# First gram by transposes, an early start for the second image's rows, three banks for the first mixing products, and weights made off VectorE

## The chip, the cores and the metric

The kernel runs on one core of a Trainium2 chip. The metric is the device time of one execution in microseconds; before the change three runs took 2819.15 to 2820.23 us, with a median of 2819.88 us. The engines are called by short names: PE is TensorE (matrix products), PEld its weight loads, DVE is VectorE, ACT is ScalarE, POOL is GpSimd, and SP issues most of the DMA transfers.

## The reference

The input x is 16 images of 64 channels with 128 x 128 pixels in float32. Four layers follow one another. Each normalizes its input over groups of two channels (`_gn`) and adds what it makes to its input:

```python
x = x + _L0_conv_ref(_gn(x), L0_conv_conv_w)    # gram over pixels, times the image, then a 1x1 convolution
x = x + _L1_conv_ref(_gn(x))                    # |Sobel x| + |Sobel y|
x = x + _L2_conv_ref(_gn(x), W, b)              # channels shifted left/right, 3x3 convolution, bias
x = x + _L3_conv_ref(_gn(x), w_bin, w1x1, b1x1, gamma, beta)  # 3x3, 1x1, batch norm over all images, clip
```

The core of layer 0 is

```python
gram = jnp.einsum('bcn,bdn->bcd', xf, xf) / N
y = jnp.einsum('bcd,bdn->bcn', gram, xf)
out = jnp.einsum('oc,bchw->bohw', conv_w, y)
```

so for each image a 64 x 64 gram matrix over its 16384 pixels is needed before any pixel of layer 0 can be made. The batch norm of layer 3 needs sums over all 16 images, so the last step over all pixels stands at the end.

## The kernel before

The work is a train of images (b = 0 to 15), each cut into NS = 8 chunks of R = 8 rows. An image lies on the 128 partitions as 64 channels times two halves of its rows. A loop over `step` (line 911), with four quarters q in each, runs the stages side by side on different images: `Front` (layer 0's product and layer 1, Sobel) starts with image 0 at step 15, `Layer2` at step 25, `Layer3` at step 35 (line 861); each image follows 8 steps behind the one before. A stage's method `at(i, q)` is called for its chunk i, which may be negative in the steps that prepare it. All instructions issued through `pe`, `dve`, `act`, `sp` and `pool` are kept in program order on their engine by the class `InOrder`, which is why nearly every instruction of the profile has line 73; one that waits holds all behind it on its engine.

**Gram** (line 407) makes the gram matrix. It loads the image as `xr`, eight tiles with the image row h on the partitions and eight channels each, in rows of 512 bytes (line 420, on SP). ACT copies each into `xw` with channels and columns exchanged (line 425). Then 128 small products on PE, one for each image column, add up the gram in PSUM (line 437), with a column of ones for the sums. A first image takes steps 0 to 9 for this. `pace` (line 871) gives the steps: image 0 from step 0, image 1 from step 12 at double speed, image 2 from step 16.

**gram_chain** (line 301) turns the gram into the mixing matrix `abd` and the coefficients `co` of the following normalization. It is a chain of tiny products and DVE instructions, a generator: each `yield` hands over, and `tick()` takes it one link further at the end of each quarter. It has two square roots on ACT (in `rstd`, line 257).

**Front** (line 450) loads x again in its own layout (line 463), mixes it by `abd` with `small_product` into one PSUM bank `po` (line 470), and ACT normalizes from there into `xh` (`prepare`, line 475). As `po` has one bank, each product waits until ACT has emptied the one before. `sobel` (line 527) is eight long DVE instructions (`u`, `e`) and two absolute values on ACT for each chunk; the first needs rows of the chunk itself and the first row of the next. For the first chunk of an image Front also stores a row of zeros from `w0` to DRAM (line 491, on SP).

**The weights** are prepared at the very start (lines 204 to 240): memsets on POOL, loads on ACT's queue, nine products `wb` x `w1` in three rounds on PE, and DVE copies and sums into `w3`, `w2`, `wm` and the packed forms `pk2`, `pk3`. The products share one region of the PSUM tile `bank`, so a round waits until the one before is copied out. The constants are loaded by SP ahead of everything (lines 118 to 133).

PSUM has the pools `ps_two` (two tiles of two banks each, for layers 2 and 3), `ps_one`, `ps_po`, `ps_g` and `ps_sm`. The SBUF pool `ring` holds `v2` (3 buffers), `v3` (2), `x3` (10), `y` and others, none of which is used before step 23.

Of the kernel before, what the change touches and what calls it, by code (L numbers as in the profile page):

```python
# [10 lines left out]
F32 = mybir.dt.float32  # L11
# [97 lines left out]
def tile_kernel(ctx: ExitStack, tc: tile.TileContext, x, cw_h, w2_t, b2, wbin_t, w1_t, b1, gamma, beta, consts, out):  # L109
# [6 lines left out]
    small = ctx.enter_context(tc.tile_pool(name="small", bufs=4))  # L116

    kc = cpool.tile([P, K_END], F32, name="kc")
    nc.sync.dma_start(kc, consts)

    def k(name):
        return kc[:, AT[name][0]:AT[name][1]]

    def load_const(src, shape, name):
        t = cpool.tile(shape, F32, name=name)
        nc.sync.dma_start(t, src)
        return t

    cwh = load_const(cw_h, [P, C], "cwh")
    b2_sb = load_const(b2, [P, 1], "b2_sb")  # L130
    b1_sb = load_const(b1, [P, 1], "b1_sb")
    gamma_sb = load_const(gamma, [P, 1], "gamma_sb")
    beta_sb = load_const(beta, [P, 1], "beta_sb")
    bn_sum = cpool.tile([P, B * NS], F32, name="bn_sum")
    bn_sq = cpool.tile([P, B * NS], F32, name="bn_sq")

# [56 lines left out]


    xw = wpool.tile([P, W // 2, C + 1, 2], F32, name="xw")
    nc.gpsimd.memset(xw[:, :, C, :], 1.0)

    xh = wpool.tile([P, 3, R + 2, W + 2], F32, name="xh")
    nc.gpsimd.memset(xh, 0.0)
    junk = wpool.tile([P, R * W], mybir.dt.bfloat16, name="junk")  # L200
    wbd = wpool.tile([P, P], F32, name="wbd")
    nc.gpsimd.memset(wbd, 0.0)

    w2 = wpool.tile([P, 3, 3, P], F32, name="w2")
    w3 = wpool.tile([P, 3, 3, P], F32, name="w3")
    nc.gpsimd.memset(w2, 0.0)
    nc.gpsimd.memset(w3, 0.0)
    for slot, i, o, ky in TO_SLOTS:
        nc.scalar.dma_start(w2[i * C:(i + 1) * C, slot, :, o * C:(o + 1) * C], w2_t[:, ky])

    wm = wpool.tile([P, 3, P], F32, name="wm")
    for n in range(2):
        o = 1 - single(TO_SLOTS, n)[0]
        nc.vector.tensor_copy(wm[:, :, cols(o)], w2[:, n, :, cols(o)])
    w0 = wpool.tile([P, P], F32, name="w0")
    nc.gpsimd.memset(w0, 0.0)

    wb = work.tile([P, R + 1, W + 2], F32, tag="u", name="wb")
    wb = flat(wb)[0:C, 0:9 * C].rearrange("p (y x c) -> p y x c", y=3, x=3)
    w1 = work.tile([P, R, W + 2], F32, tag="e", name="w1", bufs=1)[0:C, 0, 0:C]  # L220
    nc.scalar.dma_start(wb, wbin_t)
    nc.scalar.dma_start(w1, w1_t)
    for ky in range(3):
        pw = sm(3 * C, rows=C).rearrange("p (k c) -> p k c", k=3)
        for kx in range(3):
            nc.tensor.matmul(pw[:, kx, :], wb[:, ky, kx, :], w1, start=True, stop=True)
        for slot, i, o, kk in TO_PAIRS:
            if kk == ky:
                nc.vector.tensor_copy(w3[i * C:(i + 1) * C, slot, :, o * C:(o + 1) * C], pw)

    packed = {}
    for name, w, table in (("pk2", w2, TO_SLOTS), ("pk3", w3, TO_PAIRS)):
        nc.vector.tensor_add(w[:, 2], w[:, 0], w[:, 1])
        packed[name] = wpool.tile([P, 2, C], F32, name=name)
        for n in range(2):
            o, i = single(table, n)
            for kx, half in ((1, i), (0, 1 - i)):
                nc.vector.tensor_copy(
                    packed[name][half * C:(half + 1) * C, n], w[i * C:(i + 1) * C, n, kx, o * C:(o + 1) * C]
                )  # L240

    diffs, twins = {}, {}
    for name in ("d2", "d3"):
        diffs[name] = wpool.tile([P, 2, CP, W + 2], F32, name=name)
        nc.gpsimd.memset(diffs[name], 0.0)
        twins[name] = wpool.tile([P, 2, CP, W + 2], F32, name=f"q{name}")
        nc.gpsimd.memset(twins[name], 0.0)


    chains = []  # L250
# [50 lines left out]
    def gram_chain(b, pg):  # L301
# [77 lines left out]
            yield  # L379
        pk = sm(1)  # L380
        small_product(pk, pp.rearrange("p s c -> p (s c)"), k("q"))
        yield
        bias = sv("bias")
        dve.tensor_copy(bias, av[:, 2:3])
        st1 = sv("st1", 2)
# [18 lines left out]
        dve.tensor_copy(co[:, 3:4], mean)  # L404
        lead[b] = abd, co

    class Gram:
        first, last = 0, NS + 1

# [3 lines left out]
        def at(self, i, q):  # L413
            b = self.b
            CG = C // 8
            if i < NS:
                if q == 0 and i != 1:
                    for m in range(i + (1 if i == 2 else 2) if i else 0, min(i + 3, NS)):
                        t = xin.tile([P, CG, W], F32, tag="xr", name=f"xr_{b}_{m}", bufs=3)
                        sp.dma_start(t, x[b].rearrange("c h w -> h c w")[:, m * CG:(m + 1) * CG, :])  # L420
                        self.xr[m] = t

                if q == 3 and i > 0:
                    for m in (0, 1) if i == 1 else (i,):
                        act.copy(
                            xw[:, :, m * CG:(m + 1) * CG, :].rearrange("p w c t -> p c w t"),
                            self.xr.pop(m).rearrange("p c (w t) -> p c w t", t=2),
                        )
                return
            n = 4 * (i - NS) + q  # L430
            if n == 0:
                self.pg = ps_g.tile([P, CP, W], F32, tag="g", name=f"pg_{b}")[:, 0, 0:C + 1]

            for _ in range(22 if n < 4 else 20 if n < 6 else 0):
                w = self.w
                s = w % 2
                pe.matmul(
                    self.pg[s * C:(s + 1) * C, :], xw[:, w // 2, 0:C, s], xw[:, w // 2, :, s],
                    start=(w < 2), stop=(w >= W - 2),
                )  # L440
                last[0] = s
                self.w += 1
            if n == 6:
                chains.append(gram_chain(b, self.pg))
# [5 lines left out]
    class Front:  # L450
# [17 lines left out]
            self.xs[i] = t  # L468

        def mix(self, i, g):  # L470
            po = ps_po.tile([P, CP, W], F32, tag="po", name=f"po_{self.b}_{i}_{g}")
            small_product(po, self.abd, self.xs[i][:, g * CP:(g + 1) * CP, :])
            self.po[i, g] = po

# [8 lines left out]
        def at(self, i, q):  # L483
            b = self.b
            if q == 0:
                if i == -3:

                    self.xe = xin.tile([P, W], F32, tag="xe", name=f"xe_{b}", bufs=1)
                    sp.dma_start(self.xe[lo], x[b][:, HH, :])
                    sp.dma_start(self.xe[hi], x[b][:, HH - 1, :])  # L490
                    sp.dma_start(x2_d[b][0:W].rearrange("(p w) -> p w", p=1), w0[0:1, 0:W])
                if i + 3 < NS:
                    self.load(i + 3)
                if -1 <= i < NS - 1:
                    self.prepare(i + 1, 1)
                if 1 <= i:
                    self.store(i - 1)
                    act.activation(
                        junk.rearrange("p (j w) -> p j w", w=W), self.x2.pop(i - 1), AF.Square,
                        accum_out=self.st[:, 1, i - 1:i],  # L500
                    )
                if i == NS:
                    chains.append(coefficients(self.st, lambda co: coefs2.update({b: co}), b2_sb))
# [360 lines left out]
    def run(stage, b, i, q):  # L864
        if 0 <= b < B and stage.first <= i <= stage.last:
            if (stage, b) not in live:
                live[stage, b] = stage(b)
            live[stage, b].at(i, q)


    pace = {}
    at = 0
    for b in range(B):
        half = 1 <= b <= 2 * EARLY
        pace[b] = at, 2 if half else 1

        at += (NS // 2 if half else NS) + {0: 4, 2 * EARLY: 2}.get(b, 0)
    last_one = NS * (B - 1) + starts[0][1]
    steps = last_one + NS + 1

# [27 lines left out]
            loaded.append((yt, rt))  # L908
            fetched[0] += 1

    for step in range(steps):
        for q in range(4):
            for b in range(B):

# [11 lines left out]
            for b in range(B):  # L926
                at, n = pace[b]
                for m in range(n):
                    v = 4 * n * (step - at) + n * q + m
                    run(Gram, b, v // 4, v % 4)  # L930
            tick()

            if step == last_one - NS and q == 0:
# [99 lines left out]
```

## Time and profile before

| What | us |
|---|---|
| median of three runs | 2819.88 |
| the profiled execution | 2818.68 |
| its span, first to last instruction | 2816.9 |
| PE busy in the span | 2237.6 (79%) |
| DVE busy | 2201.0 (78%) |
| ACT busy | 2121.1 (75%) |
| POOL busy | 887.5 (32%) |
| eight copies xw<-xr of the first image, each | 1.15 |
| last of these copies starts | 25.66 |
| square root table load on ACT | 26.82 |
| abd of image 0 ready | about 45.5 |
| Sobel of chunk 0, first to last DVE instruction | 60.15 to 69.84 |
| Sobel of chunk 1 | 69.84 to 79.54 |

The span is cut by the page into 40 slices of 70.4 us; a digit is the busy share of an engine in tenths. The row PEclk is the granted clock of PE in tenths. In a timeline a row is one instruction, or several alike one after another: start, length, engine, line, operation, what it writes and reads, how often, and in brackets how long the engine was idle ahead of it and what ended that. DMA rows show when the transfers were issued, with the engine's queue (SPq, ACTq, POOLq).

In the whole span the chip moved 685.95 MB at a mean of 244 GB/s; from the 33rd slice on, where only the last step over all pixels is left, it moved about 420 GB/s. Between 110 and 170 us or so only Front and the next images' grams run; layers 2 and 3 join at steps 25 and 35.

### The profile page before, as it was taken

What the parts mean: (1) busy time and instruction counts of PE and PEld (TensorE: products, weight loads), DVE (VectorE), ACT (ScalarE), POOL (GpSimd) and SP (SyncE); (2) the same over time, 40 slices, a digit from 0 to 9 for tenths busy, and PEclk for the clock granted to TensorE, in tenths of its full rate; (3) what the DMA queues carried; (4) which work ended last, traced back from release to release, by engine and by line L of the source; (5) the groups of instructions that cost most, each with busy time, mean ns of one, the idle gap of its engine ahead of it and who ended that gap; (6) DMA issues with size and microseconds to landing.
All of it is one profiled execution on the core that took longest, in us unless ns stands there. A gap on an engine that the chain in (4) does not pass through costs nothing. (4 is left out here: it accounts for less than half of the span.)

```text
span 2816.9 us, 46299 instructions
## 1 busy us (share of the span) xinstructions
PE 2237.6 (79%) x14772; PEld 1153.6 (41%) x14772; DVE 2201.0 (78%) x3758; ACT 2121.1 (75%) x3171; POOL 887.5 (32%) x1326
## 2 busy tenths in 40 slices
PE   4568899999999999999999999999999995000000
PEld 2323444545554545353635363466666542000000
DVE  3999999898989898989898989999997435333332
ACT  4666779888888888888888888998997668333332
POOL 1035433343434343434343434454444310000000
PEclk7679999999999999999999999999999998555555
DMA  6789978888888888888888877787877767999999
GB/s 167 193 221 228 236 192 241 214 229 207 229 208 225 217 220 215 219 218 218 217 219 213 226 182 193 206 212 202 216 207 189 208 195 266 419 420 420 420 420 391
DMA packets 688880, 685.95 MB, mean 244 GB/s; under 512 B 61744, under 2 KB 590144, under 8 KB 688640
## 3 DMA queue, kind: packets, MB, share of 16 engines
q1 hardware_dynamic: 662656, 614.42, 73.6%
q0 software_dynamic: 24576, 68.12, 9.9%
q8 instruction: 119, 1.95, 0.3%
q14 instruction: 121, 0.99, 0.1%
q10 hardware_dynamic: 1408, 0.46, 0.1%
HBM read 346.23 MB, written 268.44 MB: 218 GB/s over the span
## 5 line engine op out<-in xcount | busy, mean ns | idle before, releaser
L73 PE MATMUL two<-d,w 128*64 128x508 f32 (+2 forms) x2560 | 889.8, 586 | 0.0
L73 PE MATMUL two<-d,wi 128*64 128x508 f32 (+3 forms) x1536 | 618.4, 577 | 0.0
L73 POOL DMA_DIRECT2D qd<-d x512 | 270.3, 530 | 867.1 <-issue 324.6
L73 PE MATMUL two<-qd,pk 128*64 128x512 f32 (+1 forms) x1024 | 518.9, 588 | 3.7 <-DMA qd<-d 3.0
L73 POOL TENSOR_SCALAR edges<-v,co 64x8 f32<-64x8 f32 x512 | 353.9, 691 | 357.5 <-ACT v L73 244.8
L73 PEld LDWEIGHTS two<-d,w 128*64 128x64 f32 x2560 | 303.3, 136 | 281.0 <-issue 200.3
L73 PE MATMUL po<-x,abd 128*64 128x512 f32 x1024 | 368.9, 631 | 60.6 <-ACT xh L73 60.6
L73 DVE TENSOR_TENSOR d<-v 128x512 f32<-128x512 f32 (+1 forms) x512 | 346.3, 679 | 75.5 <-issue 36.3
L73 PE MATMUL one<-v,w 128*64 128x508 f32 (+2 forms) x1600 | 391.8, 578 | 0.0
L73 PE MATMUL one<-v,wi 128*64 128x508 f32 (+3 forms) x1536 | 390.1, 593 | 0.0
L73 ACT COPY qd<-d 64x512 f32<-64x512 f32 x512 | 315.2, 616 | 21.0 <-DVE d L73 14.5
L73 DVE SCALAR_TENSOR_TENSOR e<-e 128x1032 f32<-128x1032 f32 (+1 forms) x256 | 313.0, 1223 | 0.0
L73 ACT ACTIVATE xh<-po,co 128x128 f32<-128x128 f32 (+1 forms) x480 | 275.3, 621 | 39.3 <-PE po L73 37.2
L73 PEld LDWEIGHTS two<-d,wi 128*64 128x64 f32 x1536 | 194.6, 135 | 146.2 <-issue 100.2
L73 DVE SCALAR_TENSOR_TENSOR y<-two,c 128x1024 f32<-128x1024 f32 x128 | 155.9, 1218 | 122.8 <-ACT v L73 65.8
L73 POOL TENSOR_SCALAR v<-v,kc 128x9 f32<-128x9 f32 x256 | 247.3, 980 | 12.0
L73 PEld LDWEIGHTS one<-v,w 128*64 128x64 f32 x1600 | 169.4, 137 | 160.4 <-issue 99.5
L73 ACT ACTIVATE v<-x,co 128x512 f32<-128x512 f32 (+2 forms) x368 | 234.8, 704 | 0.0
L73 PEld LDWEIGHTS one<-v,wi 128*64 128x64 f32 x1536 | 162.3, 138 | 154.9 <-issue 113.0
L73 ACT ACTIVATE u<-u 128x1024 f32<-128x1024 f32 x128 | 135.5, 1058 | 97.3 <-DVE u L73 96.8
L73 DVE SCALAR_TENSOR_TENSOR u<-xh 128x1170 f32<-128x1170 f32 x128 | 175.5, 1371 | 12.2 <-ACT xh L73 9.8
L73 PEld LDWEIGHTS pg<-xw 128*64 128x64 f32 x4096 | 161.6, 143 | 46.4 <-issue 38.6
(154 smaller groups left out, 3424.7 us busy)
## 6 DMA issues: line engine op xcount, KB each, us to landing
xr<-in_x SPq DMA_DIRECT2D x128, 512.0 KB, 6.9
x<-in_x SPq DMA_DIRECT2D x256, 256.0 KB, 4.2
x_d<-u SPq DMA_DIRECT2D x512, 128.0 KB, 3.6
y_d<-y SPq DMA_DIRECT2D x512, 128.0 KB, 4.2
x_d<-x SPq DMA_DIRECT2D x496, 128.0 KB, 2.5
qd<-d POOLq DMA_DIRECT2D x256, 130.0 KB, 3.0
qd<-d POOLq DMA_DIRECT2D x256, 129.8 KB, 3.7
v<-x_d SPq DMA_DIRECT2D x448, 72.1 KB, 3.0
```

The lines of the kernel that those rows point to most:

```text
L73: return self.tc.keep_in_program_order(call(*args, **kwargs))
```

## The change

The first image's gram leaves `Gram` and is made by a new function, `first_gram`, ahead of the loop. It loads the image with channels on the partitions in rows of 4 KB, transposes 128 x 128 blocks on PE into the two tiles of `ps_two`, copies these into `xw` with DVE and ACT, a half each, and runs the gram products of a chunk behind the transposes of the next. Behind it on SP come Front's first loads, then the eight `xr` tiles of the second image, in buffers of the ring `x3`. Then the chain of image 0 runs in one go, and behind five of its links ACT copies the second image's first five `xr` tiles. The loop starts at step 13; the other three copies come in step 15.

```diff
+    def first_gram():
+        pg = ps_g.tile([P, CP, W], F32, tag="g", name="pg_0")[:, 0, 0:C + 1]
+        src = []
+        t = sv("sd")
+        dve.memset(t, 1.0)
+        act.activation(t, t, AF.Sqrt)
+        for m in range(NS):
+            t = ring.tile([P, 2, CP, W], F32, tag="x3", name=f"x_first_{m}", bufs=NS + 2)
+            t = t.rearrange("p a j w -> p (a j w)")
+            for h in range(2):
+                sp.dma_start(t[h * C:(h + 1) * C], halves(x[0].rearrange("c h w -> (c h w)"), h, m * R, R))
+            src.append(t)
+        for m in range(NS + 1):
+            if m < NS:
+                two = ps_two.tile([P, 2, CP, W], F32, tag="two", name=f"turned_{m}").rearrange("p a j w -> p (a j) w")
+                for j in range(R):
+                    pe.transpose(two[:, j], src[m][:, j * P:(j + 1) * P], k("I"))
+                for h, copy in ((0, dve.tensor_copy), (1, act.copy)):
+                    copy(xw[:, m * R:(m + 1) * R, 0:C, h], two[:, :, h * C:(h + 1) * C])
+            if m > 0:
+                for w in range(2 * R * (m - 1), 2 * R * m):
+                    gram_product(pg, w)
+        run(Front, 0, Front.first, 0)
+        live[Front, 0].load(1)
+        for m in range(NS):
+            t = ring.tile([P, C // 8, W], F32, tag="x3", name=f"xr_1_{m}", bufs=NS + 2)
+            sp.dma_start(t, x[1].rearrange("c h w -> h c w")[:, m * C // 8:(m + 1) * C // 8, :])
+            rows.append(t)
+        for link, _ in enumerate(gram_chain(0, pg)):
+            if link in (2, 3, 4, 5, 6):
+                rows_to_columns(1, link - 2, rows[link - 2])
```

`gram_product` and `rows_to_columns` are the product of line 437 and the copy of line 425, put into functions. In the chain, the pause behind the product `pk` is left out for images 0 and 1.

Of the first mixing products two go to tiles of `ps_two`:

```diff
-            po = ps_po.tile([P, CP, W], F32, tag="po", name=f"po_{self.b}_{i}_{g}")
+            if self.b == 0 and (i, g) in ((0, 1), (1, 0)):
+                po = ps_two.tile([P, 2, CP, W], F32, tag="two", name=f"po_0_{i}_{g}")[:, 0]
+            else:
+                po = ps_po.tile([P, CP, W], F32, tag="po", name=f"po_{self.b}_{i}_{g}")
```

The weights' products, copies and sums go into step 16, with the copies on ACT (out of PSUM) and POOL instead of DVE; the two sums stay on DVE:

```diff
+                if kk == ky:
+                    act.copy(w3[i * C:(i + 1) * C, slot, :, o * C:(o + 1) * C], pw)
...
+            pool.tensor_copy(wm[:, :, cols(o)], w2[:, n, :, cols(o)])
...
+    for step in range(starts[2][1] - 2, steps):
...
+            if step == starts[2][1] and q < 3:
+                rows_to_columns(1, NS - 3 + q, rows[NS - 3 + q])
+            if step == starts[2][1] + 1 and q == 1:
+                weights_of_layer_3()
+                other_weights()
```

The constants' first 128 columns (the identity) are loaded by SP, the rest of the constants, all other small inputs and the layer 2 weights (six loads) by POOL, between its memsets, in this order:

```diff
+    pool.memset(xw[:, :, C, :], 1.0)
+    sp.dma_start(kc[:, 0:P], consts[:, 0:P])
+    pool.dma_start(kc[:, P:K_END], consts[:, P:K_END])
+    for t, src in ((wb, wbin_t), (w1, w1_t), (cwh, cw_h)):
+        pool.dma_start(t, src)
+    pool.memset(wbd, 0.0)
+    pool.memset(w3, 0.0)
+    pool.memset(xh, 0.0)
+    pool.memset(w2, 0.0)
+    for t, src in ((b2_sb, b2), (b1_sb, b1), (gamma_sb, gamma), (beta_sb, beta)):
+        pool.dma_start(t, src)
     for slot, i, o, ky in TO_SLOTS:
+        pool.dma_start(w2[i * C:(i + 1) * C, slot, :, o * C:(o + 1) * C], w2_t[:, ky])
+    pool.memset(w0, 0.0)
```

behind which come the memsets of the four tiles `diffs` and `twins`. `wb` and `w1` lie in buffers of the rings `v2` and `v3` instead of `work`.

More of the change, by code (lines that the diff above doesn't have):

```diff
@@ L118, in tile_kernel, with const @@
     kc = cpool.tile([P, K_END], F32, name="kc")
-    nc.sync.dma_start(kc, consts)
     def k(name):
         return kc[:, AT[name][0]:AT[name][1]]
[L124 to L133, printed above, removed]
+    def const(shape, name):
+        return cpool.tile(shape, F32, name=name)
+    cwh = const([P, C], "cwh")
+    b2_sb, b1_sb, gamma_sb, beta_sb = (const([P, 1], n) for n in ("b2_sb", "b1_sb", "gamma_sb", "beta_sb"))
     bn_sum = cpool.tile([P, B * NS], F32, name="bn_sum")
@@ L195, in tile_kernel @@
     xw = wpool.tile([P, W // 2, C + 1, 2], F32, name="xw")
-    nc.gpsimd.memset(xw[:, :, C, :], 1.0)
-    xh = wpool.tile([P, 3, R + 2, W + 2], F32, name="xh")
-    nc.gpsimd.memset(xh, 0.0)
+    pool.memset(xw[:, :, C, :], 1.0)
+    wb = ring.tile([P, (R + 1) * W + 2], F32, tag="v2", name="wb", bufs=3)
+    wb = wb[0:C, 0:9 * C].rearrange("p (y x c) -> p y x c", y=3, x=3)
+    w1 = ring.tile([P, R + 1, W], F32, tag="v3", name="w1")[0:C, 0, 0:C]
+    sp.dma_start(kc[:, 0:P], consts[:, 0:P])
+    pool.dma_start(kc[:, P:K_END], consts[:, P:K_END])
@@ L200, in tile_kernel @@
+    for t, src in ((wb, wbin_t), (w1, w1_t), (cwh, cw_h)):
+        pool.dma_start(t, src)
     junk = wpool.tile([P, R * W], mybir.dt.bfloat16, name="junk")
     wbd = wpool.tile([P, P], F32, name="wbd")
-    nc.gpsimd.memset(wbd, 0.0)
+    pool.memset(wbd, 0.0)
     w2 = wpool.tile([P, 3, 3, P], F32, name="w2")
     w3 = wpool.tile([P, 3, 3, P], F32, name="w3")
-    nc.gpsimd.memset(w2, 0.0)
-    nc.gpsimd.memset(w3, 0.0)
-    for slot, i, o, ky in TO_SLOTS:
-        nc.scalar.dma_start(w2[i * C:(i + 1) * C, slot, :, o * C:(o + 1) * C], w2_t[:, ky])
@@ L211, in tile_kernel @@
[L211 to L214, printed above, removed]
-    w0 = wpool.tile([P, P], F32, name="w0")
[L216 to L240, printed above, removed]
+    pool.memset(w3, 0.0)
@@ L242, in tile_kernel @@
+    xh = wpool.tile([P, 3, R + 2, W + 2], F32, name="xh")
+    pool.memset(xh, 0.0)
+    pool.memset(w2, 0.0)
+    for t, src in ((b2_sb, b2), (b1_sb, b1), (gamma_sb, gamma), (beta_sb, beta)):
+        pool.dma_start(t, src)
+    for slot, i, o, ky in TO_SLOTS:
+        pool.dma_start(w2[i * C:(i + 1) * C, slot, :, o * C:(o + 1) * C], w2_t[:, ky])
+    w0 = wpool.tile([P, P], F32, name="w0")
+    pool.memset(w0, 0.0)
     diffs, twins = {}, {}
@@ L244, in tile_kernel, with weights_of_layer_3, other_weights @@
         diffs[name] = wpool.tile([P, 2, CP, W + 2], F32, name=name)
-        nc.gpsimd.memset(diffs[name], 0.0)
+        pool.memset(diffs[name], 0.0)
         twins[name] = wpool.tile([P, 2, CP, W + 2], F32, name=f"q{name}")
-        nc.gpsimd.memset(twins[name], 0.0)
+        pool.memset(twins[name], 0.0)
+    def weights_of_layer_3():
+        for ky in range(3):
+            pw = sm(3 * C, rows=C).rearrange("p (k c) -> p k c", k=3)
+            for kx in range(3):
+                pe.matmul(pw[:, kx, :], wb[:, ky, kx, :], w1, start=True, stop=True)
+            for slot, i, o, kk in TO_PAIRS:
+                if kk == ky:
+                    act.copy(w3[i * C:(i + 1) * C, slot, :, o * C:(o + 1) * C], pw)
+    wm = wpool.tile([P, 3, P], F32, name="wm")
+    packed = {}
+    def other_weights():
+        for n in range(2):
+            o = 1 - single(TO_SLOTS, n)[0]
+            pool.tensor_copy(wm[:, :, cols(o)], w2[:, n, :, cols(o)])
+        for name, w, table in (("pk2", w2, TO_SLOTS), ("pk3", w3, TO_PAIRS)):
+            dve.tensor_add(w[:, 2], w[:, 0], w[:, 1])
+            packed[name] = wpool.tile([P, 2, C], F32, name=name)
+            for n in range(2):
+                o, i = single(table, n)
+                for kx, half in ((1, i), (0, 1 - i)):
+                    pool.tensor_copy(
+                        packed[name][half * C:(half + 1) * C, n], w[i * C:(i + 1) * C, n, kx, o * C:(o + 1) * C]
+                    )
     chains = []
@@ L381, in gram_chain @@
         small_product(pk, pp.rearrange("p s c -> p (s c)"), k("q"))
-        yield
+        if b > 1:
+            yield
         bias = sv("bias")
@@ L405, in gram_chain, with gram_product, rows_to_columns @@
         lead[b] = abd, co
+    def gram_product(pg, w):
+        s = w % 2
+        pe.matmul(
+            pg[s * C:(s + 1) * C, :], xw[:, w // 2, 0:C, s], xw[:, w // 2, :, s],
+            start=(w < 2), stop=(w >= W - 2),
+        )
+        last[0] = s
+    def rows_to_columns(b, m, t):
+        act.copy(
+            xw[:, :, m * C // 8:(m + 1) * C // 8, :].rearrange("p w c t -> p c w t"),
+            t.rearrange("p c (w t) -> p c w t", t=2),
+        )
+    rows = []
+    def first_gram():
[29 more added lines that the diff above has]
+                rows_to_columns(1, link - 2, rows[link - 2])
     class Gram:
@@ L424, in at @@
                     for m in (0, 1) if i == 1 else (i,):
[L425 to L428, printed above, removed]
+                        rows_to_columns(b, m, self.xr.pop(m))
                 return
@@ L434, in at @@
             for _ in range(22 if n < 4 else 20 if n < 6 else 0):
[L435 to L441, printed above, removed]
+                gram_product(self.pg, self.w)
                 self.w += 1
@@ L491, in at @@
                     sp.dma_start(x2_d[b][0:W].rearrange("(p w) -> p w", p=1), w0[0:1, 0:W])
-                if i + 3 < NS:
+                if i + 3 < NS and i + 3 not in self.xs:
                     self.load(i + 3)
@@ L868, in run @@
             live[stage, b].at(i, q)
+    first_gram()
     pace = {}
[L872 to L877, printed above, removed]
+    at = 12
+    for b in range(1, B):
+        pace[b] = at, 2 if b <= 2 * EARLY else 1
+        at += NS // pace[b][1] + (2 if b == 2 * EARLY else 0)
     last_one = NS * (B - 1) + starts[0][1]
@@ L909, in fetch @@
             fetched[0] += 1
-    for step in range(steps):
+    for step in range(starts[2][1] - 2, steps):
         for q in range(4):
@@ L925, in tile_kernel @@
                     run(Layer2, b, step - starts[1][1] - NS * b, "last of 3")
-            for b in range(B):
+            for b in range(1, B):
                 at, n = pace[b]
@@ L929, in tile_kernel @@
                     v = 4 * n * (step - at) + n * q + m
-                    run(Gram, b, v // 4, v % 4)
+                    if b > 1 or v >= 4 * NS:
+                        run(Gram, b, v // 4, v % 4)
+            if step == starts[2][1] and q < 3:
[3 more added lines that the diff above has]
+                other_weights()
             tick()
```

## The prediction

> **What bounds the kernel now.** I read the page's forty slices first, then the timeline of the head (0 to 81 us), then the waits there; the chain of waits reaches back only to about 2310 us and says nothing of the head.
>
> ```profile
> PE   4568899999999999999999999999999995000000
> DVE  3999999898989898989898989999997435333332
> PEclk7679999999999999999999999999999998555555
> ```
>
> A slice is 70.4 us. VectorE (DVE) is full from the second slice to the thirtieth, so the middle is a train of fixed work: what starts earlier ends earlier, and nothing there can take up a shift. The diff touches the first slice, where DVE stands at 3, and steps 15 and 16 right behind it. So the question is when the first Sobel step starts, and what steps 15 and 16 then cost.
>
> ```profile
> 26.95 8.31 PE L73 MATMUL pg<-xw 128*64 128x65 f32 x204 [14.88 <-ACT xw L73]
> ...
> 37.73 0.23 DVE L73 COPY gs<-pg 128x65 f32<-128x65 f32 x1 [21.26 <-PE pg L73]
> ...
> 41.20 0.88 PE L73 MATMUL bank<-kc,vv 128*2 128x128 f32 x4 [1.90 <-DVE vv L73]
> ...
> 48.69 0.20 ACT L73 ACTIVATE sd<-var 128x1 f32<-128x1 f32 x1 [8.51 <-DVE var L73]
> 48.80 3.20 ACT L73 COPY xw<-xr 128x1024 f32<-128x1024 f32 x3
> ...
> 50.17 0.13 DVE L73 COPY co<-me 128x1 f32<-128x1 f32 x1
> ...
> 52.03 0.45 ACT L73 ACTIVATE xh<-pe,co 64x128 f32<-64x128 f32 x1
> ...
> 53.68 1.97 PE L73 MATMUL po<-x,abd 128*64 128x512 f32 x4 [3.44 <-ACT xh L73]
> ...
> 60.15 1.38 DVE L73 SCALAR_TENSOR_TENSOR u<-xh 128x1170 f32<-128x1170 f32 x1 [9.84 <-ACT xh L73]
> ```
>
> Timeline: start, length, engine, instruction, in brackets the idle time before it and what ended it. Four stretches follow one another: loads and copies to 26.95 (PE waits for the last strided copy), the first gram to 37.73 (10.8 us), its chain of small products to 50.3 (12.6 us), and 9.85 us until the first Sobel instruction at 60.15, in which one PSUM bank goes back and forth between PE (1.97 us a product) and ACT.
>
> ```profile
> 75.16 5.41 PE L73 MATMUL pg<-xw 128*64 128x65 f32 x168
> ...
> 75.83 1.07 ACT L73 ACTIVATE u<-u 128x1024 f32<-128x1024 f32 x1 [2.24 <-DVE u L73]
> ...
> 76.93 1.29 DVE L73 SCALAR_TENSOR_TENSOR u<-xh,co,u 128x1024 f32<-128x1024 f32 x1
> ...
> 80.63 0.23 DVE L73 COPY gs<-pg 128x65 f32<-128x65 f32 x1 [1.01 <-PE pg L73]
> ```
>
> Step 16 (69.84 to 79.54): DVE goes from one instruction to the next; ACT's absolute values end 0.03 us before DVE needs them. Whatever holds ACT here holds DVE.
>
> **Part 1, the gram by transposes.** Removed from the front: eight 512 KB loads in 512-byte rows, the last landing near 25.5 us, and eight copies of 1.15 us. In their place come sixteen 256 KB loads. SP issues a pair of such loads in 1.1 to 1.2 us, so the last goes out at 1.2 + 8 x 1.15 = 10.4 us; with the 4.2 us to landing of the row "x<-in_x" that is 14.6. By bytes: 4.2 MB, and 0.75 MB of constants on POOL, at 290 GB/s (a good stretch of the head) take 17 us from 1.5. Chunks end between 14.6 and 18.5, the first near 5.
>
> PE gets 64 transposes and the same 128 gram products. The products cost 10.8 us in all, 84 ns each: the 88 instructions at 117.68 took 3.86 us, half of it cold, the 168 at 75.16 took 5.41, so a product is 64 ns warm and about 108 cold. No row shows a transpose. From above: a full float32 product with 128 moving columns, half of the 1.01 us of the same two products at 92.37 (clock 0.50), 0.505 us. From below: a quarter of that, if the data goes through once, not four times, 0.126 cold and half of it warm. The weight loads at 53.68, four of 64 columns in 0.30 us, give 0.15 for 128 columns. I take 0.15, on the assumption that the data goes through once and loading it as weights is then the longest part; it is nearest to the lower row. PE: 5 + 64 x 0.15 + 10.8 = 25.4 us. The PSUM copies (512 columns, DVE and ACT at once, 0.77 us by the row xh<-po) lie behind the other chunk's products. Bounds: data alone, 18.5 and three more chunk parts of 0.7, about 20; every transpose at 0.505 and every product cold, 5 + 32.3 + 13.8 = 51.
>
> Here a page speaks against the change. The Trainium skill, "TensorE: Matmul & The Clock Gate", Part 4 (PE-mode transpose), gives about 275 ns for a 128x128 transpose in a kernel and says that transposes don't count as activity for the clock. By it the gram would end at 5 + 17.6 + 13.8 = 36.4 us, and the first part would be worth 1.3 us. No row here can confirm it; the clock rows only show that ordinary products lift it.
>
> Gain at the gram's end: 37.7 - 25.4 = **12.3** (-13 to 18).
>
> **Part 2, the chain with five copies in it.** The chain is the same, 12.6 us, so the coefficients are there at 38.0. Five copies of 1.15 = 5.75 us now stand on ACT between the two square roots, which lie 8.7 us apart (39.98 and 48.69): room enough, if the rows have landed. Each copy waits for its load; behind it on ACT stands the second root, and behind that the coefficients. The loads stand on SP behind the store x_d<-w, which reads w0; w0 is set on POOL behind 0.22 + 0.2 + 1.07 + 3.35 + 1.07 us of memsets and 14 DMA issues. At 0.53 each (the row qd<-d) w0 is ready at 14.3, at 1.0 each (192 pieces where qd has 64) near 21. Then 1.05 MB of x and 2.6 MB of five chunks at 250 GB/s, 14.6 us: the fifth lands at 29 to 36 and is copied by 30 to 37. The second root is due at 25.4 + 11.0 = 36.4. So nothing, at most 1; were the gram done at 20, up to 6 of that would be lost again.
>
> **Part 3, three banks.** Three products stand finished when the coefficients come, and the three copies at 48.80 no longer hold ACT. What remains before Sobel is ACT: 0.45 + 0.45 + 0.77 + 1.13 + 1.13 = 3.9, and 0.3 for hand-overs: 4.2, not 9.85. Gain **5.65**; at least the 1.7 us for which the copies held ACT (50.3 to 52.03), at most 6. Sobel starts at 42.2. Chunks 6 to 8 are copied in step 15, 3.5 us of ACT beside 9.7 of DVE, as before.
>
> **Part 4, the weights, moved into step 16.** In the head they cost nothing: DVE waited 21 us for the gram.
>
> ```profile
> 6.89 0.87 PE L226 MATMUL bank<-w,wb 64*64 64x64 f32 x6 [6.89 <-DMA w<-in_w_t]
> ...
> 7.87 0.73 DVE L229 COPY w<-bank 64x192 f32<-64x192 f32 x2 [7.87 <-PE bank L226]
> ...
> 8.66 0.90 PE L226 MATMUL bank<-w,wb 64*64 64x64 f32 x6 [0.90 <-DVE w L229]
> ```
>
> Three rounds: a product triple, two copies out, and only then the next triple, for one region of the bank is shared. A round was 1.77 us cold; warm with ACT's copies (0.45 each, as 64x128 out of PSUM) 0.5 + 0.9 + 0.1 = 1.5, three 4.5. They stand on PE behind the second 44 gram products of step 16, done at 75.16 + 88/168 x 5.41 = 78.0 on the old clock, so they end at 82.5. ACT's absolute values (75.83) are behind the copies, and DVE's sum into w3 waits for them too: DVE resumes at 83.6, not 76.93. Loss 6.7, less the 1.01 us that DVE idled at 80.63 anyway. DVE's two sums (0.55 each) lie in that gap; so do POOL's copies, for which nobody waits. I take **-6** (from -1, if the products slip in ahead, to -9, if rounds stay cold and ACT's copies are slower). Behind PE's rounds stand the last 40 gram products and a mixing product; both are done before DVE asks.
>
> **Small edits, at nothing.** The constants and six weight loads leave SP and ACT for POOL, whose memsets beside them nobody needs before step 25, but for w0 (part 2). The load of the square root's table (1.28 us at 26.82) goes to the front, where ACT waits for the first chunk; it was hidden before by the gram. For image 1 the chain passes its last but one product without a pause: DVE then waits some 0.5 us for PE once, inside step 20 or so. The second x chunk is loaded ahead of the chunks' rows on SP instead of behind them; 0.5 MB, 2 us, counted in part 2.
>
> **Sum.** 12.3 + 5.65 - 6 = 12. The profiled execution took 2818.68 (span 2816.9 and 1.8 around it): 2806.7. The median shown is 1.2 above it, so 2808.
>
> **Rivals.**
> (a) Transposes at a product's price, on a cold clock. For: no row shows one faster, and PE starts cold (24 instructions touched per us at 28, 38 from 32 on). Against: PE is now busy without a gap. Break-even is a gram ending at 37.4, that is (37.4 - 5 - 13.8)/64 = 0.29 us each; from 0.38 the kernel is slower by over 5.6. At 0.505 the gram ends at 51: 13.7 slower, 2834.
> (b) A middling price, 0.2 to 0.3, or rows that land late so that ACT holds the second root (w0 at 21, 215 GB/s: 4 us). Gain 1 to 7, 2813 to 2819.
> (c) The weights find cover (loss 1 to 2) and the gram is bound by data: 17 to 21 gained, 2799 to 2803. For: ACT idles 2.24 us before 75.83. Against: the program's order puts them behind 44 products.
> That the change does nothing is out: no gram in the old form is left for the first image.
>
> **Chances.** Forecast (2803 to 2812) 0.50; (a) slower 0.17, with 0.03 for another loss; (b) 0.18; (c) 0.12. A measurement can tell 0.2%, 5.6 us: faster by more takes the forecast, (c) and a quarter of (b), 0.66; within, the rest of (b), 0.14; slower 0.20. The range reaches from (c) to the end of (b): 2799 to 2820.
>
> **What would show it.** Right: the chain's first copy gs<-pg near 25 us, the second root within 11 us of it, first Sobel near 42, a DVE gap of some 6 us in step 16 before a u<-xh,co,u, all later steps alike. Wrong: transposes over 0.3 us each, ACT waiting for xr loads before the second root, or no gap in step 16.

## The result and the profile after

The changed kernel took 2811.97 us (median of nine runs, 2810.42 to 2815.58) beside 2820.23 for the kernel before (nine runs, 2817.85 to 2822.18): a ratio of 0.9972, 95% interval 0.9962 to 0.9982. That is 8.3 us faster; 12 were forecast. The profiled execution took 2810.42 us, its span was 2808.6.

The forty slices of the changed kernel, 70.2 us each:

```profile
PE   6578899999999999999999999999999995000000
DVE  4999999898989898989898989999997435333332
PEclk8679999999999999999999999999999998555555
```

The differences lie at the start: PE has 6 instead of 4 in the first slice and 7 instead of 6 in the third, DVE 4 instead of 3 in the first. The train behind looks alike. So the gain has to be found in the head. The timeline there (start, length, engine, instruction, in brackets the idle time before it and what ended it):

```profile
8.66 1.94 PE L73 MATMUL turned<-kc,x_first 128*128 128x128 f32 x8 [8.66 <-DMA x_first<-in_x]
...
10.94 1.94 PE L73 MATMUL turned<-kc,x_first 128*128 128x128 f32 x8 [0.34 <-DMA x_first<-in_x]
...
14.01 1.09 PE L73 MATMUL turned<-kc,x_first 128*128 128x128 f32 x8
...
15.04 1.23 PE L73 MATMUL pg<-xw 128*64 128x65 f32 x32
...
26.35 1.06 PE L73 MATMUL turned<-kc,x_first 128*128 128x128 f32 x8 [0.95 <-DMA x_first<-in_x]
...
28.85 1.21 PE L73 MATMUL pg<-xw 128*64 128x65 f32 x30 [0.16 <-ACT xw L73]
...
30.10 0.23 DVE L73 COPY gs<-pg 128x65 f32<-128x65 f32 x1 [1.96 <-PE pg L73]
...
38.55 1.15 ACT L73 COPY xw<-xr 128x1024 f32<-128x1024 f32 x1 [0.42 <-DMA xr<-in_x]
...
41.26 0.20 ACT L73 ACTIVATE sd<-var 128x1 f32<-128x1 f32 x1 [1.56 <-DVE var L73]
...
42.74 0.13 DVE L73 COPY co<-me 128x1 f32<-128x1 f32 x1
...
46.61 1.38 DVE L73 SCALAR_TENSOR_TENSOR u<-xh 128x1170 f32<-128x1170 f32 x1 [3.73 <-ACT xh L73]
```

Eight transposes take 1.94 us at first and 1.09 later (0.136 each, the last one's full length included), the 32 instructions of 16 gram products 1.23 (0.077 a product). The gram ends at 30.1 instead of 37.7, the coefficients are there at 42.9 instead of 50.3, and Sobel starts at 46.61 instead of 60.15: 13.5 us earlier. Step 16 then gives some of it back:

```profile
65.40 0.56 PE L73 MATMUL bank<-w,wb 64*64 64x64 f32 x6
66.00 0.65 ACT L73 COPY w<-bank 64x192 f32<-64x192 f32 x2 [5.95 <-PE bank L73]
...
66.69 0.42 PEld L73 LDWEIGHTS bank<-w,wb 64*64 64x64 f32 x6 [0.87 <-ACT w L73]
...
69.23 1.06 ACT L73 ACTIVATE u<-u 128x1024 f32<-128x1024 f32 x1
69.24 0.56 DVE L73 TENSOR_TENSOR w<-w 128x384 f32<-128x384 f32 x1 [5.37 <-ACT w L73]
...
70.33 1.28 DVE L73 SCALAR_TENSOR_TENSOR u<-xh,co,u 128x1024 f32<-128x1024 f32 x1 [0.53 <-ACT u L73]
...
72.94 0.22 DVE L73 COPY gs<-pg 128x65 f32<-128x65 f32 x1
```

ACT stood for 5.95 us until the first triple of products came, passed the bank back and forth three times, and only then made the absolute value; DVE stood 5.37 us for the last copy and 0.53 for the absolute value.

From the start of the first Sobel instruction of each step the lead over the kernel before can be followed through the train (us earlier than before, in one profiled execution each; the runs are told below):

| Kernel | step 15 | step 17 | step 19 | step 25 | near 1790 us |
|---|---|---|---|---|---|
| changed | 13.5 | 7.8 | 6.6 | 6.8 | 7.5 |
| e1, weights in the head | 12.1 | 11.0 | 10.1 | 11.0 | 8.4 |
| e2, two queues | 11.9 | 6.3 | 5.4 | 5.6 | 5.8 |
| e3, e1 and e2 | 10.2 | 10.2 | 9.3 | 9.3 | 9.6 |
| e4, one bank | 8.6 | 2.2 | 1.0 | 1.1 | 1.9 |
| e5, transposes twice | 6.7 | 1.8 | 0.6 | 1.8 | 2.6 |
| e6, copies behind the chain | 11.2 | 6.3 | 5.2 | 6.0 | 4.1 |
| e7, constants behind | 14.8 | 8.4 | 7.3 | 7.6 | 9.0 |
| e8, weights apart | 12.4 | 12.4 | 11.3 | 11.5 | 12.3 |
| e9, e7 and e8 | 14.1 | 12.7 | 11.5 | 12.2 | 9.6 |
| e10, pause restored | 11.9 | 7.0 | 6.7 | 7.9 | 4.8 |
| e11, e9 and e10 | 13.4 | 12.0 | 11.7 | 12.2 | 10.2 |

Two things are read here. Most of the lead of step 17 is still there at the end, but it wanders by one to three us on the way, mostly in jumps of a single step. Step 54 (near 650 us) takes 16.6 us in the kernel before and in e7, e9 and e11 (the three with the constants behind the image), but 17.5 to 18.3 in the changed kernel and the eight others; e10 loses 2.9 us in step 31 and e9 2.2 in step 78. And heads that are the same in the code differ: Sobel starts at 46.6 in the changed kernel, at 47.7 and 48.3 in e8 and e10, which differ from it only later. The changed kernel's profiled execution is also the fastest of its nine, that of e1 the slowest of its five. So a single profile says little on effects below 1.5 us; there the runs' medians have to be used, or an effect that comes back in several profiles.

### The profile page after: what moved, and what is told of

It is laid out like the page before. It is cut to its first block, busy times and chain, and to the rows that moved or that the text cites. A ratio compares the mean times of both kernels' runs of the same rounds, so it can differ in the third digit from the quotient of the medians.

```text
span 2808.6 us, 46444 instructions
## 1 busy us (share of the span) xinstructions
PE 2243.5 (80%) x14836; PEld 1158.4 (41%) x14836; DVE 2200.9 (78%) x3751; ACT 2116.7 (75%) x3177; POOL 893.7 (32%) x1350
## 3 DMA queue, kind: packets, MB, share of 16 engines
q8 instruction: 120, 1.97, 0.3%
## 5 line engine op out<-in xcount | busy, mean ns | idle before, releaser
L73 POOL TENSOR_SCALAR edges<-v,co 64x8 f32<-64x8 f32 x512 | 345.2, 674 | 357.0 <-ACT v L73 269.6
L73 PE MATMUL po<-x,abd 128*64 128x512 f32 x1024 | 362.2, 622 | 51.5 <-ACT xh L73 48.5
L73 ACT COPY qd<-d 64x512 f32<-64x512 f32 x512 | 315.3, 616 | 21.0 <-DVE d L73 14.6
L73 POOL TENSOR_SCALAR v<-v,kc 128x9 f32<-128x9 f32 x256 | 250.6, 992 | 11.9
```

The costliest lines, as they stand in the source:

```text
L73: return self.tc.keep_in_program_order(call(*args, **kwargs))
```

## The experiments

Each is the changed kernel with the edit named, timed beside the kernel before on the same chip. The experiments ran on several chips, and the kernel before had medians of 2819.17 to 2820.42 us there; a difference from the changed kernel, which is told as one of medians, can hold up to about 1 us of that.

**e1: the weights in the head.**

```diff
+            if m in (2, 4, 6):
+                weights_of_layer_3((m // 2 - 1,))
...
+            if m == NS - 1:
+                other_weights()
...
-            if step == starts[2][1] + 1 and q == 1:
-                weights_of_layer_3()
-                other_weights()
```

> Moves the weights of layer 3 (three rounds) and the sums and packed copies from step 16 into the first gram, one round behind chunks 2, 4 and 6, where PE waits for loads. Theory (step 16 pays for them: DVE stood 5.37 us for the last copy, and 0.53 more): step 16 shrinks from 16.63 to about 10.7 us (the 1.0 us wait for the gram product comes back), the first gram ends at most 0.6 us later, and the time falls by 5 to 6 us, to about 2806. Rival (the wait only takes the place of others that come back in steps 17 to 19): the gain at the start of step 17 is gone by step 20, time within 2 us of the changed kernel's 2812.

Measured: 2806.95 us (ratio 0.9953, 0.9940 to 0.9965), 5.0 below the changed kernel. DVE's steps are whole again: from 57.71 to 69.63 step 16 has no gap but 2.1 us for the gram product at its end. The gram ends at 31.6, 1.5 later: PE had less time to give away than thought. The price of the weights in step 16 is shown; the rival, that later waits would take the gain back, is out for steps 17 to 25. Near 1790 us this profile leads the changed kernel's by only 0.9 us more; for the whole train the runs have to speak, and all five lie below the changed kernel's nine.

**e8: the weights apart.** The nine products go to step 15, into a tile with a place for each round; copies and sums stay in step 16.

```diff
+    def products_of_layer_3():
+        two = ps_two.tile([P, 2, CP, W], F32, tag="two", name="weights_3").rearrange("p a j w -> p a (j w)")
+        for ky in range(3):
+            at = two[0:C, ky // 2, (ky % 2) * 3 * C:(ky % 2 + 1) * 3 * C]
...
+            if step == starts[2][1] and q == 1:
+                products_of_layer_3()
```

> The weights of layer 3 stay behind the head, but their nine products go ahead, into step 15, into a tile of ps_two with a place for each round, and only the six copies and the sums stay in step 16, so no engine passes a bank back and forth. Theory (the loss in step 16 is the passing and the place behind 44 gram products, not the work): DVE's wait in step 16 falls from 5.9 to under 1 us, the first Sobel instruction stays at 46.6, time 5 to 6 us lower, 2806 to 2807, or 1 us below the run with the weights in the head. Rival (the copies' 2 us on ACT are the loss wherever they stand): 3 us lower at most.

The timeline of step 16 in e8:

```profile
61.03 1.93 ACT L73 COPY w<-weights 64x192 f32<-64x192 f32 x6
...
64.48 1.10 DVE L73 TENSOR_TENSOR w<-w 128x384 f32<-128x384 f32 x2
...
65.50 1.27 DVE L73 SCALAR_TENSOR_TENSOR u<-xh,co,u 128x1024 f32<-128x1024 f32 x1
```

The same six copies, 1.93 us, now lie in ACT's free time, and DVE has no wait at all; the lead of step 15 is whole at step 17 (12.4 and 12.4). Measured: 2807.60 us (0.9957, 0.9944 to 0.9969), 4.4 below the changed kernel. So not the work was the loss, but the passing of one bank and the place in the order. The two aren't told apart by this run, which changes both; in the changed kernel's trace ACT waits 5.95 us for the first triple and then needs 3.2 (66.00 to 69.23) for three rounds in which it copies for 1.92.

**e7: the constants behind the image.**

```diff
-    pool.dma_start(kc[:, P:K_END], consts[:, P:K_END])
-    for t, src in ((wb, wbin_t), (w1, w1_t), (cwh, cw_h)):
-        pool.dma_start(t, src)
...
             src.append(t)
+        sp.dma_start(kc[:, P:K_END], consts[:, P:K_END])
+        for t, d in ((cwh, cw_h), (wb, wbin_t), (w1, w1_t)):
+            sp.dma_start(t, d)
```

> The 0.7 MB of constants and weights that POOL loads at the start go behind the first image's loads, on SP. Theory (the first transposes start at 8.66 us, not 5, because these loads share the engines with the first chunk; after that PE is busy without a gap for 20 us): first transpose at 5.5 to 6.5, gram's end 2 to 3 us earlier, at 27 to 28, time 2 to 3 us lower, about 2809.5. Rival (the loads' total bytes bind, or the first loads are late by themselves): first transpose within 1 us of 8.66, time 2812.

The timeline of e7's head:

```profile
6.01 1.94 PE L73 MATMUL turned<-kc,x_first 128*128 128x128 f32 x8 [6.01 <-DMA x_first<-in_x]
...
28.22 0.23 DVE L73 COPY gs<-pg 128x65 f32<-128x65 f32 x1 [1.96 <-PE pg L73]
...
38.95 1.15 ACT L73 COPY xw<-xr 128x1024 f32<-128x1024 f32 x1 [0.34 <-DMA xr<-in_x]
39.99 0.19 ACT L73 ACTIVATE sd<-var 128x1 f32<-128x1 f32 x1
```

The first chunk is there 2.65 us earlier, the gram ends 1.9 earlier. Now the fifth copy waits for its load until 38.95 and the second root runs straight behind it: the wait that the prediction priced for an early gram. The coefficients come 1.3 us earlier, not 1.9. In e9 and e11, told below, which hold the same edit, the gram ends at 28.2 and 28.4 too, but the fifth copy starts at 39.68 and 40.34 and the coefficients are there at 42.3 and 43.0: late rows take back most of what the early gram gave. Measured: 2809.18 us (0.9969, 0.9957 to 0.9981), 2.8 below the changed kernel; 0.8 of that is the difference between the kernel before in the two sets of runs, and the intervals overlap. So the time alone doesn't show the gain; the earlier first chunk and gram, which all three profiles with this edit have, are shown.

**e2: two queues.** `sp.dma_start` becomes `(sp, act)[h].dma_start` for the first image's loads.

> The first image's loads of the lower 64 partitions stay on SP's queue, those of the upper 64 go to ACT's, so that both halves are in flight together. Theory A (the first gram is bound by its loads, and these are slow, about 245 GB/s, because each fills only 64 partitions at a time): last chunk lands by 22 instead of 26.3 us, first gram ends near 26 to 27 instead of 30.1 (then PE's 2.3 us a chunk bind), time 3 us lower, about 2809. Rival B (PE's transposes and products bind): the loads come earlier, the gram's end stays within 0.5 us. Rival C (the 16 engines are simply full with what is in flight): loads and gram end stay within 0.5 us, time 2812.

Measured: 2815.21 us (0.9979, 0.9969 to 0.9988), 3.2 above the changed kernel. None of the three was right, for a reason that none named. The timeline of e2:

```profile
2.12 11.86 ACTq L73 DMA_DIRECT2D x_first<-in_x x6
...
14.02 1.13 ACT L73 COPY xw<-turned 128x512 f32<-128x512 f32 x2 [11.79 <-DMA x_first<-in_x]
...
14.69 1.99 PE L73 MATMUL pg<-xw 128*64 128x65 f32 x30 [1.64 <-ACT xw L73]
```

The first chunk is there at 6.11, but ACT can't leave its eight issues before 14, and its copies stand behind them in its order. The last three go out at 9.81, 11.80 and 13.51, each 0.02 to 0.03 us behind the landing of an earlier load of ACT's queue (9.79, 11.78, 13.48). From 14.69 on PE had its work without a gap above 0.15 us and no wait for a load, and ended at 31.7. So from there PE alone sets the end, and earlier loads don't help.

**e3: both of e1 and e2.**

> Both of the two runs before together. If both theories hold, the gains add: 8 to 9 us below the changed kernel, about 2803. If only the weights matter, 2806; if only the queues, 2809.

Measured: 2810.84 us (0.9963, 0.9950 to 0.9975). The two add, 5.0 gained and 3.2 lost, within 0.7 us; the forecast's sign for the queues was wrong.

**e5: each transpose twice.** `for j in range(R)` becomes `for j in [j for j in range(R) for _ in range(2)]`.

> The changed kernel with each of the 64 transposes issued twice, into the same place. Theory (from 8.66 us on PE binds the first gram: transposes of 0.136 us and products of 0.077, 2.2 us a chunk): each chunk takes 1.09 us more, less the 1.5 us that PE waited, so the gram's end goes from 30.1 to 37 to 40 and the time rises by 7 to 9 us, to about 2820. Rival (the loads bind, one chunk in 2.2 us): gram's end at most 3 us later, time at most 2815. The first 32 transposes now run ahead of any product: if transposes by themselves lift PE's clock, their pace goes from 0.24 to 0.14 us inside these 32, some 4 us behind the first; if they don't, it stays at 0.24 until products have run.

The timeline of e5:

```profile
8.79 6.37 PE L73 MATMUL turned<-kc,x_first 128*128 128x128 f32 x32 [8.79 <-DMA x_first<-in_x]
15.09 1.23 PE L73 MATMUL pg<-xw 128*64 128x65 f32 x32
16.25 1.97 PE L73 MATMUL turned<-kc,x_first 128*128 128x128 f32 x16
...
36.20 0.23 DVE L73 COPY gs<-pg 128x65 f32<-128x65 f32 x1 [1.96 <-PE pg L73]
```

The gram ends 6.1 us later and Sobel starts 6.8 later; 2816.47 us (0.9989, 0.9980 to 0.9999), 4.5 above the changed kernel. Both sizes are below what was expected, the gram's end by 1 us and the time by 2.5; but it is twice what the rival allows for the gram. So PE binds the first gram for most of the way. The step that the expectation had too dear is the price of a further transpose: eight more in a chunk take 0.88 us (1.97 against 1.09), not 1.09, so 64 take 7.0; PE's waits for loads in the changed kernel, 1.5 us, are gone here and hold a part of it. The 32 transposes ahead of any product change their pace on the way, as two shorter windows of the same timeline show (8.7 to 14.14 and 14.6 to 15.1):

```profile
8.79 5.57 PE L73 MATMUL turned<-kc,x_first 128*128 128x128 f32 x25 [8.79 <-DMA x_first<-in_x]
...
14.34 0.82 PE L73 MATMUL turned<-kc,x_first 128*128 128x128 f32 x6
```

The first 25 start 0.21 us apart, the last six 0.11. The pace doubles near 14.3 us, 5.5 behind the first transpose and 0.8 ahead of the first product: transposes alone had lifted the clock.

**e4: one bank.** The condition on `(i, g)` becomes `False`.

> The changed kernel with a single PSUM bank for the first mixing products again. Theory (three banks are worth the passing of one bank between PE and ACT): from the coefficients to the first Sobel instruction 3.7 us become 7 to 8.5 (the copies that held ACT for 1.7 us stay in the chain), time 3.5 to 5 us higher, about 2816. Rival (the stretch is bound by ACT alone, or the second x loads are late anyway): under 1 us.

The timeline of e4 behind its coefficients (43.4 us):

```profile
45.08 1.98 PE L73 MATMUL po<-x,abd 128*64 128x512 f32 x4 [1.71 <-ACT xh L73]
...
48.28 1.98 PE L73 MATMUL po<-x,abd 128*64 128x512 f32 x4 [1.23 <-ACT xh L73]
...
51.54 1.38 DVE L73 SCALAR_TENSOR_TENSOR u<-xh 128x1170 f32<-128x1170 f32 x1 [8.11 <-ACT xh L73]
```

A product, its emptying, the next product: 8.1 us from the coefficients to Sobel where three banks take 3.7. Measured 2816.02 us (0.9987, 0.9978 to 0.9996), 4.05 above the changed kernel. The theory held.

**e6: the copies behind the chain.** The five calls of `rows_to_columns` go to the ends of the quarters from step 13, q = 3, to step 14, q = 3.

> The changed kernel with the five copies of the second image's rows taken out of the chain and put at the ends of the quarters of steps 13 and 14. Theory (in the chain they stand in ACT's free time and cost nothing; outside they stand between the normalizations): coefficients unchanged within 0.3 us of 12.8 us behind the gram, from there to the first Sobel instruction 3.7 becomes up to 9 us (five copies of 1.15), time 3 to 5 us higher, about 2816. Rival (copies in the chain hold the second square root): coefficients 0.5 to 1 us earlier, the sum of both stretches unchanged, time within 1 us of 2812.

Measured: the coefficients 12.4 us behind the gram instead of 12.8, Sobel 6.8 behind them instead of 3.7; 2814.03 us (0.9981, 0.9972 to 0.9989), 2.1 above the changed kernel. The copies in the chain cost it 0.4 us and save 3:

```profile
48.92 1.38 DVE L73 SCALAR_TENSOR_TENSOR u<-xh 128x1170 f32<-128x1170 f32 x1 [6.83 <-ACT xh L73]
```

The theory held in kind, at the low end of its size or below.

**e9: e7 and e8 together.**

> Constants behind the first image's loads, and the products of the weights ahead in step 15. If both theories hold, the gains add: 7.5 to 8.5 us below the changed kernel, 2803.5 to 2804.5, 0.6% below the kernel before. If only the weights do, 2806.

Measured: 2806.81 us (0.9956, 0.9943 to 0.9968), 5.2 below the changed kernel, not 7.5 to 8.5. The lead at step 25 was 12.2 us, about what the parts add up to there (6.8 of the changed kernel, 4.7 more in e8, 0.8 more in e7); near 1790 us it was 9.6. So the gains add up to step 25, though that of e7 is small by then; the train took 2.6 us of this execution's lead, 2.2 of them in step 78. Why is open.

**e10: the pause restored**, `if b > 0` for `if b > 1` behind the product `pk`.

> The changed kernel with the pause behind the product pk kept for image 1. Theory (DVE waits once for PE there, inside step 18): the lead over the kernel before, which falls from 7.5 to 6.6 us between the starts of steps 18 and 19 and stays there at step 25, stays at 7.3 to 7.8 instead; time 0.5 to 1 us lower, within what runs can tell. Rival (the fall comes from the later phase of the second gram's chain against Sobel): lead at step 25 within 0.2 us of 6.85.

Measured: the lead stays at 6.7 between steps 18 and 19 and grows to 7.9 at step 25, where the changed kernel falls from 7.5 to 6.6 and 6.8; 2811.45 us (0.9971, 0.9960 to 0.9981). Between the starts of steps 18 and 19 all ten profiles without the pause lose 0.8 to 0.9 us, and the two with it, e10 and e11, lose nothing. In the trace the pause is worth that, in the time it can't be told from nothing.

**e11: e9 and e10 together.**

> Constants behind the first image's loads, products of the weights ahead in step 15, and the pause behind pk kept for image 1. Theory (three losses of the head that have nothing to do with one another): the start of step 17 leads the kernel before by 12 to 13 us, as with the first two, and step 25 by 12.5 to 13.5, 0.5 to 1 us more than with the first two; time 2804 to 2806. Rival (the train of later steps takes leads over some 9 us back): lead at step 25 over 12 us, but under 10 at the last Sobel step, time 2806 to 2808.

Measured: 2804.93 us (0.9947, 0.9934 to 0.9961), the fastest of all, 7.0 below the changed kernel. Step 17 leads by 12.0 and step 25 by 12.2, no more than in e9. The pause's part is there between steps 18 and 19 (11.7 and 11.7, where e9 falls from 12.4 to 11.5), but by step 25 nothing of it is left over e9; near 1790 us 10.2 was left, close to what the rival expects, while the time lies in the theory's range. What can be said is that it beats both kernels, and that e1, e8, e9 and e11 lie within 2.7 us of one another.

## Why the prediction was right, and what was mis-sized

The forecast of a gain of 0.2% or more held, and the time, 2811.97, lies in the range of 2799 to 2820, but at the very edge of the band of 2803 to 2812 that got half of the chance. Of the signs that it named, the second root within 11 us of the gram's end (11.2) and the gap of some 6 us in step 16 (5.9) came; a gram near 25 us (30.1) and a first Sobel near 42 (46.6) did not. Point by point:

- **Which stretches decide.** Right: all of the difference is made between 0 and 75 us, and the train passes it on. That nothing there can change a shift was too strong; the lead wandered between 5.3 and 8.7 us behind step 17.
- **Part 1, 12.3 forecast, 7.6 measured.** This is the step that was mis-sized, and in it the term "the first near 5": the first chunk was there at 8.66. The sum has no working for the 5; its own 4.2 us to landing, counted from the issue of the pair's second load at 1.8, would have given 6.0. With POOL's large loads out of the way (e7) just that is seen, with all sixteen loads in the queue: the second load lands 4.1 us behind its issue and the first transpose starts at 6.01. So 1.0 us is a slip in the sum, and the other 2.65 are POOL's 0.75 MB beside the first chunk; a later load of the sixteen took 7.7 to 11.2 us in the changed kernel. The end of the loads was mis-sized too: 14.6 to 18.5 us at 290 GB/s were forecast, and at 225 to 246 GB/s the last one landed at 26.3. That cost little, since PE was busy meanwhile: it waited 1.5 us for loads (at 10.94, 20.83 and 26.35) and 0.16 for a copy (at 28.85), 1.6 in all, for which the sum had no term. PE's own work was a little less than forecast: 30.1 - 8.66 - 1.6 = 19.8 us against 20.4. Together 3.7 + 1.6 - 0.6 = 4.7, which is the whole miss.
- **The price of a transpose.** Right: 0.15 was taken and 0.136 measured warm, 0.24 cold, as a mean over eight. Here the page on the clock was weighed against the rows. The usual duration of the instruction in this trace is what the page gives:

```profile
L73 PE MATMUL turned<-kc,x_first x64: 272/273/447, 8.7 to 27.1; 128*128 128x128 f32 x64
```

  (least, median and most ns of the 64.) But behind one another eight take 1.09 us, since the next begins before the last ends. The Trainium skill, "TensorE: Matmul & The Clock Gate", Part 4 (PE-mode transpose), states some 275 ns for a bf16 transpose in a kernel, which agrees as a duration of these float32 ones and would be twice too long as a price. It also states that transposes don't lift the clock, which the 32 transposes of e5 contradict. The measurement decides: the gram ended 6.3 us ahead of the 36.4 that the prediction had worked out from the page, and that sum started from a first chunk at 5, not 8.66.
- **The PSUM copies** were thought to run on DVE and ACT at once; they ran one behind the other (0.69 + 0.63), but PE's other chunk hid all but 0.16 us.
- **Part 2, nothing to 1 us.** Right: 0.4 by e6. The second root waited for DVE, not for rows. But this is in part luck: the fifth copy was forecast to be done by 30 to 37, and its load held it until 38.55. It cost nothing because the gram, and with it the root, came almost 5 us later than forecast. With the gram 2 us earlier the root does wait for rows, as e7 shows.
- **Part 3, 5.65 forecast, 6.1 measured** (9.85 to 3.7). e4 and e6 test its two parts one at a time: without the banks 4.4 us are lost up to Sobel, without the copies' move 3.1. Together that is more than 6.1, so the parts overlap.
- **Part 4, -6 forecast, -5.8 measured** (13.5 to 7.8 from step 15 to step 17). DVE resumed 23.7 us behind the first Sobel instruction; the sum had 83.6 - 60.15 = 23.45. e1 and e8 confirm the cause.
- **Small edits.** The pause at `pk` was put at 0.5 us in step 20 or so; it cost 0.8 to 0.9, between the starts of steps 18 and 19.
- **Rival (a)** falls with the price of a transpose. **(b)** gave nearly the right time, but not for its reasons: neither transposes of 0.2 to 0.3 us nor a held root made the difference. **(c)** is not what happened, but e8 shows that its cover for the weights exists, if they are put there.

Open is why single steps of the train, above all step 54, take longer in some executions, and so why the lead wanders.

## What to carry to other kernels

A load's time to landing holds only with the bytes that were in flight when it was read: the first pair took the 4 us of the row when POOL's large loads were put behind the image, and its chunk was there 2.65 us later beside them. Count the bytes of every queue. Work moved out of an idle head into a full step costs what it makes the full engine wait, not its own length; here two microseconds of copies cost six behind other products and through one shared bank, and nothing with the products made a step ahead and a place for each round. A DMA issued by an engine that also computes can hold that engine: in e2 the last of ACT's eight issues went out only as earlier loads landed.

## What the hardware showed that was not expected

The loads in 4 KB rows into 64 partitions were slower than those in 512-byte rows into 128. In windows of the changed kernel (columns: stretch, length, busy time and count of PE, PEld, DVE, ACT, POOL, then granted clock, DMA share, GB/s), the first stretch has the former (with some small loads by POOL among them), the second the latter:

```profile
14.00:20.00 6.00, 6.00 (x110) 5.35 (x108) 1.87 (x3) 1.55 (x3) 3.49 (x6) 1.00 1.07 225
...
34.00:40.00 6.00, 2.92 (x25) 1.88 (x23) 3.08 (x16) 4.50 (x4) 0.00 (x0) 0.50 1.06 311
```

The engines are full in both, at 225 and 311 GB/s. Splitting the partitions' halves over two queues (e2) gave 293 GB/s from 8 to 14 us, where the changed kernel had 246, but 225 again from 14 to 20; what limits these loads isn't settled, and as they differ in size and row length too, the number of partitions isn't shown to be the reason. And the clock column reads 1.00 through the first 32 us, while the pace of transposes doubles at 13 us: ahead of its first change the column doesn't show the clock. The trace's first record of the clock is that rise, at 12.97 us (14.31 in e5).
